# Two attention layers on one core: the third score before a block's first mixing, the last mixing after the seventh score, and 64 columns in the product of the row sums

## The chip, the cores and the metric

The kernel runs on one NeuronCore of a Trainium2 chip. The metric is the device time of one execution in microseconds. Four compute engines work side by side and are tied together by semaphores: TensorE (matrix products, PE in the profile), VectorE (DVE), ScalarE (ACT) and GpSimd (POOL). SyncE (SP) issues most of the transfers.

## The reference

The input is x of shape (8, 512, 32, 32): eight images of 512 channels and 1024 tokens. Two residual layers follow one another, each behind a group normalization; the second, the one touched here, mixes the heads before the softmax and normalizes the attention after it:

```python
attn = jnp.einsum('bhdq,bhdT->bhqT', q, k) * scale      # 8 heads, hd = 64
attn = jnp.einsum('gh,bhqT->bgqT', w_head, attn)        # mixing of the heads
attn = jax.nn.softmax(attn, axis=-1)
mean = jnp.mean(attn, axis=(-2, -1), keepdims=True)
var = jnp.var(attn, axis=(-2, -1), keepdims=True)
attn = (attn - mean) / jnp.sqrt(var + EPS)
attn = attn * in_gamma[None, :, None, None] + in_beta[None, :, None, None]
out = jnp.einsum('bhqT,bhdT->bhqd', attn, v)
```

All of it is in fp32.

## The kernel before, in words

The first layer runs for all eight images, then the second layer, one image after another (the loop `for b in range(B)`, line 1892). Only the second layer's class `Attention1` (from line 1616) is changed.

An image's 1024 queries are cut into eight blocks of 128; `p` counts them. For one block the work goes through five stages, each on another engine:

- **Scores** (`scores(p, i)`, line 1624), i from 0 to 7: four head pairs (`hp = i % 4`) for each half of the keys (`kh = i // 4`). Four matmuls on 64x64 tiles of the array fill one two-bank PSUM tile of the pool `ps1_m`; ScalarE (VectorE for odd i of block 0) copies it into the tile `raw[kh]`. The pool `rawpool` has two buffers, one for each half of the keys, so a block's first copy needs the buffer that the previous block's first half leaves.
- **Regrouping** (`regroup(kh, s)`, line 1645): two transfers of 256 KB on SP's queue carry a slice s of `raw[kh]` into the tile `re`, where all heads of a query lie next to each other on the partitions. `re` exists once, with four slices s; a slice is overwritten only when the mixing that reads it is done. The slices of a second key half need all of its four score copies, the eighth score's among them.
- **Mixing** (`mix(p, s)`, line 1658): sixteen matmuls on 32x32 tiles with the weights `wmix` fill two PSUM tiles of the same pool `ps1_m`. Two exponentials on ScalarE (line 1675), one for each tile, write the tile `e` (two buffers, pool `epool1`).
- **Transpose and moments** (`flip`, line 1680, `moments`, line 1692): VectorE transposes `e` into `et` and takes `bn` statistics of it. An `e` buffer is free when its moments are done.
- **Values** (`values(p, u, ...)`, line 1702): matmuls with `et` as the moving operand and 64 columns of `v` as weights on 128x64 tiles, four parts for each half u; `leave` (line 1722) copies the result out on ScalarE.

`sums` (line 1735) turns the `bn` statistics into the row sums and the sums of squares, `totals` (line 1745) adds them over partitions with two products against the selection matrix `sel`, and `reciprocals` (line 1755) goes on from there; it reads the first 32 rows of the result only.

The pool `ps1_m` has three buffers of two banks, which scores, mixings and projections take in turn; a group waits until the tile three places before it has been read. The values and the sums use the pool `ps1_a`, two buffers of one bank.

The order on each engine is the order in which the program calls its instructions (the schedule is set by hand, line 576). Per block there are four steps t (`step`, line 1838). In step t of block p the scores of block p, the mixing t of block p - 1 and values of block p - 2 (in step 3 of block p - 1) are interleaved. "First mixing" means `mix(p - 1, 0)`, in step 0; "last mixing" means `mix(p - 1, 3)`, in step 3. Step 8, after an image's last block, mixes block 7 and has no scores. Regroupings are issued at the end of a step: slices 0 and 1 of the first key half in step 1, slice 2 in step 2, slice 3 of the first half and then all four of the second half in step 3. An agenda (`ag.run`) places other work between: loads of the next image's input and weights (`piece`, `left_k`, `y` in the profile), its normalization at block 5, its projections in the last block.

Of the kernel before, what the change touches and what calls it, by code (L numbers as in the profile page):

```python
# [9 lines left out]
F32 = mybir.dt.float32  # L10
# [8 lines left out]
P = 128  # L19
# [448 lines left out]
def tile_two_attention_layers(  # L468
# [19 lines left out]
    nc = tc.nc  # L488
    B, C, T = x_d.shape
    H = w_head.shape[0]  # L490
    D = C // H
# [24 lines left out]
    def const_tile(name, shape, dt=F32):  # L516
        return const.tile(shape, dt, tag=name, name=name)
# [45 lines left out]
    sel = const_tile("sel", [P, 32])  # L563
# [130 lines left out]
    with ExitStack() as l0:  # L694
# [5 lines left out]
        stat = l0.enter_context(tc.tile_pool(name="stat", bufs=2))  # L700
# [368 lines left out]
        def attention0(b, agenda):  # L1069
# [96 lines left out]
            for i in range(0, NI + 2, 2):  # L1166
                if i < NI:
                    scores(i)
                    scores(i + 1)
                if i >= 2:  # L1170
                    for w in (i - 2, i - 1):
                        values(w)
                        sums(w)
                    if (i - 1) % NG == NG - 1:
                        g = (i - 1) // NG
                        agenda.at(i + 2, lambda g=g: totals(g))
                        agenda.at(i + 6, lambda g=g: reciprocals(g))
                        agenda.at(i + 10, lambda g=g: finish(g))
                agenda.run(i)
                agenda.run(i + 1)  # L1180
# [83 lines left out]
    with ExitStack() as l1:  # L1264
# [6 lines left out]
        stat = l1.enter_context(tc.tile_pool(name="stat1", bufs=2))  # L1271
# [5 lines left out]
        def acc_psum(nm):  # L1277
            return ps_a.tile([P, FB], F32, tag="a", name=nm)

        def m_psum(nm):  # L1280
            return ps_m.tile([P, 2, FB], F32, tag="m", name=nm)
# [163 lines left out]
        def k_leave():  # L1445
            for fn in due:
                fn()
            due.clear()
# [167 lines left out]
        class Attention1:  # L1616
# [41 lines left out]
            def mix(self, p, s):  # L1658

                b = self.b  # L1660
                ps = [m_psum(f"m1_{b}_{p}_{s}_{h}") for h in range(2)]
                for c in range(4):
                    for a in range(4):
                        rows = slice(a * 32, a * 32 + 32)
                        nc.tensor.matmul(  # L1665
                            ps[a // 2][c * 32 : c * 32 + 32, a % 2].rearrange(
                                "p (r kb k) -> p r kb k", r=2, k=32
                            ),
                            wmix[rows].rearrange("p g i -> p (g i)"),
                            re_t[rows, s].rearrange("p r (kb c k) -> p c r kb k", c=4, k=32)[:, c],  # L1670
                            start=True, stop=True, tile_position=(a * 32, c * 32),
                        )
                e = self.e[p, s] = epool.tile([P, 2, 4, 2 * P], F32, tag="e", name=f"e1_{b}_{p}_{s}")
                for h in range(2):
                    nc.scalar.activation(  # L1675
                        e[:, :, 2 * h : 2 * h + 2].rearrange("p r a k -> p a r k"),
                        ps[h].rearrange("p a (r k) -> p a r k", r=2), AF.Exp,
                    )

            def flip(self, p, s):  # L1680

                u, st = s // 2, s % 2
                if st == 0:
                    self.et[p, u] = etpool.tile(
                        [P, 8, 16, H, 4], F32, tag="et", name=f"et_{self.b}_{p}_{u}"
                    )
                nc.vector.transpose(  # L1687
                    self.et[p, u].rearrange("p kb (r st a) g q -> p st kb r (a g q)", r=2, st=2)[:, st],
                    self.e[p, s].rearrange("p r a (kb k) -> p kb (r a) k", k=32),
                )  # L1690
# [44 lines left out]
            def sums(self, p):  # L1735

                bn = self.bn.pop(p).rearrange("p s a (r k) -> p r (s a) k", k=3)
                zz = stat.tile([P, 2, 2, 16], F32, tag="zz", name=f"zz_{self.b}_{p}")
                mean, m2 = bn[..., 1], bn[..., 2]
                nc.vector.tensor_scalar_mul(zz[:, 0], mean, float(2 * P))  # L1740
                nc.vector.tensor_mul(zz[:, 1], mean, zz[:, 0])
                nc.vector.tensor_add(zz[:, 1], zz[:, 1], m2)
                self.zz = zz

            def totals(self, p):

                ps = acc_psum(f"z1_{self.b}_{p}")
                for m in range(2):
                    nc.tensor.matmul(
                        ps[:32, ts(m, 32)], self.zz[:, m].rearrange("p r c -> p (r c)"), sel,  # L1750
                        start=True, stop=True,
                    )
                self.reciprocals(p, ps)
# [84 lines left out]
            def step(self, p, t, ag):  # L1838

                new, old, older = p < NT, p >= 1, p >= 2  # L1840
                if t == 3 and old:
                    self.mix(p - 1, 3)
                if new:
                    self.scores(p, 2 * t)
                    if t == 0:
                        self.scores(p, 1)
                if t == 0 and older:
                    self.values(p - 2, 0, 2, 3)
                    self.leave(p - 2, 0)
                    self.sums(p - 2)  # L1850
                    if p % 2 == 0 and p >= 4:
                        self.divide(p // 2 - 2, nc.gpsimd)
                if t in (1, 2) and older:
                    self.values(p - 2, 1, t - 1)
                    if t == 1:
                        self.flip(p - 1, 0)
                        self.totals(p - 2)
                        self.moments(p - 1, 0)
                if t == 3 and old:
                    self.values(p - 1, 0, 0)  # L1860
                if new and t:
                    self.scores(p, 2 * t + 1)
                if t == 3 and old:
                    self.values(p - 1, 0, 1)
                if t < 3 and old:
                    self.mix(p - 1, t)
                ag.run(4 * p + t - 0.5)
                if t == 2 and older:
                    self.values(p - 2, 1, 2, 3)
                    self.leave(p - 2, 1)  # L1870
                k_leave()
                if p == 1 or old and t:
                    self.flip(p - 1, t)
                    self.moments(p - 1, t)
                if new:
                    for kh, s in (
                        (), ((0, 0), (0, 1)), ((0, 2),), ((0, 3), (1, 0), (1, 1), (1, 2), (1, 3)),
                    )[t]:
                        self.regroup(kh, s)
                if old and t == 0:  # L1880
                    self.piece(4 if p < 5 else 5)
                ag.run(4 * p + t)
# [155 lines left out]
```

## Time and profile before

| | us |
|---|---|
| median of three runs (4051.15 to 4058.64) | 4051.75 |
| the profiled execution | 4059.13 |
| its span, first to last instruction | 4057.0 |

| engine | busy us | share of the span |
|---|---|---|
| PE | 3927.5 | 97% |
| DVE | 2834.4 | 70% |
| ACT | 1969.0 | 49% |
| POOL | 128.7 | 3% |

The second layer's scores begin at 1800.6 us, and its last mixings end near 4000 us. The products of the row sums (line 1749) are 256 records of the form 128*32, in 64 groups; the mixings 8192 records of the form 32*32; the second layer's scores 4096 of the form 64*64; the values 16384 of the form 128*64. Each matmul of the program is two records. How to read it: a busy time is the sum of the durations of an engine's instructions, and a busy PE may still be waiting inside; idle time is laid to the releaser that came last by the semaphores, which can be another than the one named. Lines are those of the kernel before.

### The profile page before, as it was taken

The numbers are of one execution on the slowest core, as the hardware profiler recorded it, in microseconds if no ns is written. First come the engines' busy times: TensorE is split into PE (matmuls) and PEld (weight loads), VectorE is DVE, ScalarE is ACT, GpSimd is POOL, SyncE is SP. The second block draws the span as 40 slices with busy tenths as digits, with TensorE's granted clock in tenths as the row PEclk, the third lists the DMA queues.
The fourth block names the chain that finished last, engine by engine and source line by source line (L and its number), as shares of the span: only waits on it lengthen the run. The fifth ranks groups of instructions, "written<-read, shape, count | busy, mean of one in ns | idle before, by whom it ended". The sixth has DMA issues, their size and how long they took to land. (4 is left out here: it accounts for less than half of the span.)

```text
span 4057.0 us, 96037 instructions
## 1 busy us (share of the span) xinstructions
PE 3927.5 (97%) x41932; PEld 1817.7 (45%) x41932; DVE 2834.4 (70%) x4124; ACT 1969.0 (49%) x2431; POOL 128.7 (3%) x150
## 2 busy tenths in 40 slices
PE   8999999999999999999999999999999999999997
PEld 4353535353444435334444534544444444445344
DVE  4748475756666575748849859769679679498596
ACT  1727263545445363516617427347257166174273
POOL 0000000000000000000000001001000000000010
PEclk9999999999999999999999999999999999999998
DMA  3313131211111111228738639559469287386384
GB/s 124 114 47 115 45 118 48 87 50 59 60 66 66 68 53 60 77 83 208 182 120 220 189 105 234 155 143 231 128 174 233 78 216 194 114 223 193 104 212 121
DMA packets 268636, 519.12 MB, mean 128 GB/s; under 512 B 49840, under 2 KB 84912, under 8 KB 261552
## 3 DMA queue, kind: packets, MB, share of 16 engines
q1 hardware_dynamic: 261664, 497.96, 42.9%
q0 software_dynamic: 6544, 14.94, 1.6%
q8 instruction: 331, 5.42, 0.6%
q14 instruction: 97, 0.79, 0.1%
HBM read 197.16 MB, written 46.92 MB: 60 GB/s over the span
## 5 line engine op out<-in xcount | busy, mean ns | idle before, releaser
L1687 DVE STREAM_TRANSPOSE et<-e 128x2048 f32<-128x2048 f32 x256 | 586.7, 2292 | 133.8 <-ACT e L1675 127.6
L1714 PEld LDWEIGHTS a<-et,v 128*64 128x64 f32 x16384 | 509.4, 138 | 287.2 <-issue 215.8
L1698 DVE BATCH_NORM_STATS2 bn<-e 128x6 f32<-128x512 f32 x1024 | 633.5, 673 | 0.0
L1086 ACT ACTIVATE e<-s 128x1024 f32<-128x1024 f32 x512 | 497.2, 1026 | 233.9 <-PE s L1081 233.4
L1675 ACT ACTIVATE e<-m 128x1024 f32<-128x1024 f32 x512 | 496.3, 1021 | 208.4 <-issue 102.1
L1643 ACT COPY raw<-s 128x1024 f32<-128x1024 f32 x480 | 475.0, 1019 | 229.6 <-PE s L1631 193.1
L1714 PE MATMUL a<-et,v 128*64 128x64 f32 x16384 | 557.3, 225 | 5.8 <-DVE et L1687 5.1
L1631 PE MATMUL s<-k,q 64*64 64x512 f32 x4096 | 541.7, 615 | 9.7 <-DVE q L1497 3.1
L1094 DVE TENSOR_TENSOR zacc<-zacc,e 128x1024 f32<-128x1024 f32 x384 | 468.8, 1221 | 93.8 <-ACT e L1086 71.8
L1081 PE MATMUL s<-q,k 64*64 64x512 f32 x4096 | 490.1, 593 | 2.3 <-ACT e L1086 2.3
L1107 PE MATMUL a<-e,v 64*64 64x512 f32 x4096 | 484.1, 589 | 0.0
L1665 PE MATMUL m<-re,wmix 32*32 32x512 f32 x8192 | 334.9, 611 | 72.6 <-DMA re<-raw 60.7
L1107 PEld LDWEIGHTS a<-e,v 64*64 64x64 f32 x4096 | 156.7, 133 | 282.8 <-issue 282.5
L1081 PEld LDWEIGHTS s<-q,k 64*64 64x64 f32 x4096 | 147.9, 133 | 275.2 <-issue 240.7
L1631 PEld LDWEIGHTS s<-k,q 64*64 64x64 f32 x4096 | 118.0, 132 | 259.2 <-issue 85.0
L1458 PE MATMUL pv<-wv,y 128*128 128x512 f32 x480 | 212.1, 597 | 0.0
L1730 ACT COPY q<-a 64x256 f32<-64x256 f32 x256 | 93.7, 366 | 158.9 <-PE a L1714 156.3
L1665 PEld LDWEIGHTS m<-re,wmix 32*32 32x32 f32 x8192 | 71.6, 103 | 215.5 <-ACT raw L1643 88.3
L1763 POOL DMA_DIRECT2D zd<-rz x56 | 34.7, 619 | 3492.5 <-DMA y<-x 1858.2
L1458 PEld LDWEIGHTS pv<-wv,y 128*128 128x128 f32 x480 | 89.3, 190 | 117.4 <-issue 109.5
L1462 ACT COPY v<-pv 128x512 f32<-128x512 f32 x30 | 17.6, 585 | 218.4 <-PE pv L1458 218.4
L1092 DVE TENSOR_TENSOR zacc<-e,e 128x1024 f32<-128x1024 f32 x64 | 78.3, 1223 | 55.3 <-ACT e L1086 55.3
(315 smaller groups left out, 3936.8 us busy)
## 6 DMA issues: line engine op xcount, KB each, us to landing
re<-raw SPq DMA_DIRECT2D x1024, 256.0 KB
left_q<-left_q SPq DMA_DIRECT2D x17, 1792.0 KB
left_p<-left_p SPq DMA_DIRECT2D x17, 1792.0 KB
left_k<-left_k SPq DMA_DIRECT2D x10, 1792.0 KB
x<-in_x_dram SPq DMA_DIRECT2D x32, 512.0 KB
rzb<-zd SPq DMA_DIRECT2D x128, 128.0 KB
x<-x SPq DMA_DIRECT2D x64, 256.0 KB
left_v<-left_v SPq DMA_DIRECT2D x8, 1792.0 KB
```

Of the source, the lines that this page charges most:

```text
L1081: nc.tensor.matmul(ps[c * D : c * D + D, m], k[r, hp, k0 : k0 + D], q[r, hp, ts(f, FB)], start=True, stop=True,)
L1086: nc.scalar.activation(e[i], ps, AF.Exp, scale=S0 * S0)
L1094: nc.vector.tensor_add(zacc[g], zacc[g], e[i])
L1107: nc.tensor.matmul(acc[g][a][m * D : m * D + D], v[rows, kc, ts(2 * hp + m, D)], e[i][rows, m], start=(kc == 0), stop=(kc == NG - 1),)
L1458: nc.tensor.matmul(ps[:, m], y_t[b][:, c, ts(2 * i + m, P)], w[:, c], start=(c == 0), stop=(c == NCC - 1),)
L1631: nc.tensor.matmul(ps[c * D : c * D + D, m], qo_t[b][r, p, hp, ts(c, D)], k_t[b][r, hp, ts(kh, FB)], start=True, stop=True,)
L1643: nc.scalar.copy(dst, ps)
L1665: nc.tensor.matmul(ps[a // 2][c * 32 : c * 32 + 32, a % 2].rearrange("p (r kb k) -> p r kb k", r=2, k=32), wmix[rows].rearrange("p g i -> ...
L1675: nc.scalar.activation(e[:, :, 2 * h : 2 * h + 2].rearrange("p r a k -> p a r k"), ps[h].rearrange("p a (r k) -> p a r k", r=2), AF.Exp,)
L1687: nc.vector.transpose(self.et[p, u].rearrange("p kb (r st a) g q -> p st kb r (a g q)", r=2, st=2)[:, st], self.e[p, s].rearrange("p r a ( ...
L1698: nc.vector.bn_stats(self.bn[p][:, s, a], e[:, :, a].rearrange("p r k -> p k r"))
L1714: nc.tensor.matmul(acc[two * D : two * D + D, s].rearrange("p (x q) -> p x q", q=4), v_t[b][:, kb, ts(g, D)], et[:, kb, :, g], start=(kb = ...
```

## The change

Three things change in `Attention1`.

1. In `step`, the third score `scores(p, 2)` is called in step 0, right after the first two and ahead of the values, the output copies and the first mixing. In step 1 no score stands at the beginning any more.
2. In step 3, the seventh score `scores(p, 6)` is called before the last mixing, and no longer after it. The mixing issues its first exponential itself and hands back its second one, which step 3 calls after the eighth score (and its copy). In the other steps the second exponential follows at once, as before.
3. The tile `zz` gets a third part that repeats the first one. The two products of `totals` take two neighbouring parts as weights, 64 columns where there were 32, and write 64 rows of PSUM where they wrote 32; the additional rows are not read.

```diff
@@ mix @@
-                for h in range(2):
+
+                def exponentials(h):
                     nc.scalar.activation(
                         e[:, :, 2 * h : 2 * h + 2].rearrange("p r a k -> p a r k"),
                         ps[h].rearrange("p a (r k) -> p a r k", r=2), AF.Exp,
                     )
+
+                exponentials(0)
+                return lambda: exponentials(1)
@@ sums @@
-                zz = stat.tile([P, 2, 2, 16], F32, tag="zz", name=f"zz_{self.b}_{p}")
+                zz = stat.tile([P, 3, 2, 16], F32, tag="zz", name=f"zz_{self.b}_{p}")
                 mean, m2 = bn[..., 1], bn[..., 2]
-                nc.vector.tensor_scalar_mul(zz[:, 0], mean, float(2 * P))
+                nc.vector.tensor_scalar_mul(
+                    zz[:, 0::2], mean.unsqueeze(1).to_broadcast([P, 2, 2, 16]), float(2 * P)
+                )
@@ totals @@
-                        ps[:32, ts(m, 32)], self.zz[:, m].rearrange("p r c -> p (r c)"), sel,
+                        ps[:D, ts(m, 32)],
+                        self.zz[:, m : m + 2].rearrange("p m r c -> p (m r c)"), sel,
@@ step @@
-                if t == 3 and old:
-                    self.mix(p - 1, 3)
-                if new:
+                if new and t != 1:
                     self.scores(p, 2 * t)
                     if t == 0:
                         self.scores(p, 1)
+                        self.scores(p, 2)
+                if t == 3 and old:
+                    second = self.mix(p - 1, 3)
...
                 if new and t:
                     self.scores(p, 2 * t + 1)
                 if t == 3 and old:
+                    second()
                     self.values(p - 1, 0, 1)
                 if t < 3 and old:
-                    self.mix(p - 1, t)
+                    self.mix(p - 1, t)()
```

## The prediction

> **What bounds the kernel now.** I read the page first, then the waits of each engine from 1830 us on (the second layer, the only part touched), then the timeline of one query block. From the page:
>
> ```profile
> PE   3927.5 (97%) x41932; PEld 1817.7 (45%) x41932; DVE 2834.4 (70%) x4124; ACT 1969.0 (49%) x2431; POOL 128.7 (3%) x150
> ```
>
> TensorE is the bound, so what can be won is its idle time and the slots that its groups take. Waits, as engine, line, releaser, total us, times, longest:
>
> ```profile
> PE m L1665 <- DMA re<-raw: 60.7, 45, 4.4
> PE m L1665 <- ACT q L1730: 7.5, 9, 0.9
> ...
> ACT e L1675 <- DVE bn L1698: 38.8, 44, 2.0
> ```
>
> The idle time that matters is one place: the mixing waits for the regrouped scores (`re`). The timeline puts every one of these waits at a block's first mixing. Eight stand after an image's last block (2.63 to 4.39, sum 25.7), where no scores are left. Thirty-seven (35.0) stand between two blocks; the nine laid to `q` (7.5) and two more of 0.5 and 0.6 are the same place: 43.6 us over 48 intervals, 0.91 each. That it is not the `q` copy shows in other blocks, where the mixing starts before that copy ends.
>
> One interval, S being the eighth score (start us, us, engine, what):
>
> ```profile
> 3931.32 1.14 PE L1665 MATMUL m<-re,wmix 32*32 32x512 f32 x32
> 3932.39 1.10 PE L1631 MATMUL s<-k,q 64*64 64x512 f32 x8
> 3933.09 1.94 ACT L1675 ACTIVATE e<-m 128x1024 f32<-128x1024 f32 x2 [0.83 <-DVE bn L1698]
> 3934.51 1.09 PE L1631 MATMUL s<-k,q 64*64 64x512 f32 x8
> 3934.92 1.94 ACT L1643 COPY raw<-s 128x1024 f32<-128x1024 f32 x2
> 3936.61 1.95 PE L1631 MATMUL s<-k,q 64*64 64x512 f32 x16
> 3938.28 1.93 ACT L1643 COPY raw<-s 128x1024 f32<-128x1024 f32 x2 [1.42 <-PE s L1631]
> 3941.38 1.15 PE L1665 MATMUL m<-re,wmix 32*32 32x512 f32 x32 [0.81 <-ACT q L1730]
> 3942.46 1.09 PE L1631 MATMUL s<-k,q 64*64 64x512 f32 x8
> ...
> 3944.68 2.31 DVE L1687 STREAM_TRANSPOSE et<-e 128x2048 f32<-128x2048 f32 x1 [1.76 <-ACT e L1675]
> ```
>
> S = 3934.51. The eighth copy ends at S+2.36, and the first mixing (M) starts at S+6.87: 4.5 us from copy to landed data. PE's own work from S fills only 6.06. VectorE still idles 1.76 before its first transpose. Interval M to M: 21.93; without the wait 21.1.
>
> **What the skill says.** TensorEngine Tiling (Array Packing), Key Properties: a change of tiling mode drains TensorE. The trace agrees: two adjacent scores start 0.86 apart, while a score followed by another mode takes a slot of 1.02: 0.16 per change. Perfetto Trace Analysis, DMA Instruction — HWDGE: the semaphore follows a confirmed write, so there is delay after the last byte that no issue order shortens; the 4.5 us for two 256 KB copies agree. TensorE: Matmul & The Clock Gate, Part 1: idleness of about 3.4 us halves the clock. Here 2.21 us sufficed at 2237.95, where the clock reads 0.61 and then 0.54, and three slots took 4.8 us for 3.2.
>
> **The change, part by part.**
>
> *Third score before the first mixing.* It issues four matmuls (eight records) and one copy; no DMA, since regrouping stays in its step, so SP and POOL see nothing move. PE's work from S to M grows from 6.06 by 0.86 to 6.9. The data are due at S+6.7 (copy ending at S+2.2, below, plus 4.5), so the typical wait goes: minus 43.6. The score joins two others, and one mode change goes: 56 blocks x 0.16 = minus 9.0.
>
> Behind the moved copy on ScalarE stand the output copies (0.74) and then the first exponentials. The three copies start when the raw buffer is free, which needs the regroup of slice 3 landed. Today the copies start at S+3.25 to S+4.87, mean about 3.75. That regroup waits for the last mixing, which now ends about 1.0 later; I shift the copies by the whole of it, although a backlog of transfers may already set the landing. For a copy now at S+c: the second copy (whose PSUM the mixing takes) ends at S+c+3.0, the exponentials start at S+c+4.66. With M at S+7.25 (6.9 and the 0.28 below, rounded up) the first delays M where c > 4.25, the second the exponentials where c > 3.92 (they start 1.33 after M). Over the 48 values of c this gives 2.0 + 3.8: plus 6. The second mixing takes PSUM from these exponentials and has no slack left, so I count that lag in full.
>
> *Last mixing after the seventh score, second exponential after the eighth copy.* PE has as many mode changes as before. ScalarE's order becomes copy 7, exponential, copy 8, exponential. The exponentials wait for `bn` (an e buffer): today they start near S-1.4 and push copy 8 to S+2.36; then only one stands ahead, and copy 8 follows S directly, ending at S+2.17. The new wait: the second exponential ends at S+2.17+0.97 = 3.14, and the next block's second score takes its PSUM. PE would reach it at S+1.02+1.08+0.86 = 2.96, ScalarE releases it at about 3.24: 0.28 x 48 = plus 13.4. The fourth transpose waits for the same exponential; VectorE reaches it at S+3.0 today and nearer S+4 in the new order (S comes 1.02 sooner after M), so it costs nothing while `bn` covers it; uncovered, at most 0.2 per block.
>
> *Sums with 64 columns.* Values run as 128*64, the sums as 128*32: one mode change goes. No run shows this product at 64 columns. Ends: a full change saved, 64 x 0.16 = minus 10; or nothing saved and four wider weight loads at the values' 138 ns for 106, plus 0.03 x 4 x 64 = plus 8. I take 0.10 each, minus 6.4: the mode then equals its neighbour's. The VectorE product writes 64 elements instead of 32 (0.19 us now); 0.02 to 0.06 more, hidden in the idle 1.76 before the transpose.
>
> *What stays.* Three intervals wait 2.2 to 2.5, not by copy 8 but because the transfers are late (M at S+8.25, 8.27, 8.58): about 1.1 of each stays, plus 3.3. In seven images one interval carries normalisation, and VectorE has no idle time (M = 2521.99: no wait before the transpose); those cannot shorten by the full 0.6: plus 4. The eight waits after the last block stay. The half-clock stretch may vanish (1.6); not counted.
>
> Sum: -43.6 - 9.0 - 6.4 + 6 + 13.4 + 3.3 + 4 = -32.3. The profiled execution took 4059.1 (span 4057.0 and 2.1 around it), so 4027; the median of the runs shown is 7.4 below it: 4051.75 - 32 = 4020.
>
> **The rivals.**
>
> A. *Transfers bind.* In 2425 to 2560 us the DMA engines' share is 0.91, or 20.0 us per 21.95 us interval. In block 2206 they idle about 2 us while SP waits for copy 8; if that gap stays, nothing shortens by more than a few tenths. For it: six images carry extra loads in these blocks. Against it: the last image has a share of 0.82 to 0.87, and the same interval and wait, so latency sets it. Gain about 0.25 x 48 = 12: 4040, down to none.
>
> B. *The second exponential costs nothing* and the sums save all: 32 + 13 + 4 = 49 less: 4003.
>
> C. *Slower: copies pile up ahead of the exponentials.* If the slice-3 regroup lands much later than the shift I used, M waits for the second copy and the second mixing for the exponentials. An interval gains 0.91 + 0.26 - 0.28 = 0.89 before this. A copy at today's c = 4.9 costs 0.65 + 0.33, so the change decides to slower where the landings average 1.1 us beyond my shift. At 1.6 beyond (c = 5.35): 1.1 + 0.33 = 1.43, net 0.54 x 48 = 26 slower: 4078. For it: c reaches 4.87 today. Against it: the mean is 3.75.
>
> That nothing changes because the compiler's order is kept is excluded: the order is written out by hand.
>
> **How the numbers follow.** Forecast 0.58 (own range 4006 to 4034), A 0.19, B 0.12, C 0.11. A measurement of this kernel can tell 0.2%, 8 us. Of A, 0.07 falls within that of no change; faster is 0.58 + 0.12 + 0.12 = 0.82, slower C's 0.11. The range takes B's end and A without its weakest part: 4000 to 4046; outside it are C and some 0.07.
>
> **What would show it.** Right: first mixings between blocks without a wait of more than 0.3 typically; a new PE wait of score on `e` of 0.2 to 0.4 at a block's second score, some 48 times; copy 8 ending at S+2.2; sums in form 128*64; intervals near 21.3. A: those waits stay on DMA with the share at 0.95 or more. C: mixings wait on ACT `raw`, the second mixing on `e`, by over a microsecond. The prediction fails most easily in the 4.5 us from copy 8 to landed data, and in the landing of slice 3, both set by transfers that I can only shift, not derive.

## The result, and the profile after

The kernel after takes 4035.18 us (median; 4032.16 to 4037.43), the kernel before 4054.68 in the same comparison: a ratio of 0.9952 with an interval of 0.9937 to 0.9966, some 19 us faster. The forecast was 4020 with a range of 4000 to 4046: the sign was right, the gain less than two thirds of what was expected. The profiled execution after took 4037.07 (span 4035.0), the one before 4059.13 (span 4057.0).

The page of the kernel after, busy time of each engine:

```profile
PE 3929.8 (97%) x41932; PEld 1825.9 (45%) x41932; DVE 2836.2 (70%) x4124; ACT 1976.2 (49%) x2431; POOL 129.1 (3%) x150
```

TensorE is as busy as before while the span is 22 us shorter. A busy PE can wait inside its rows, as will be seen. The waits of TensorE from 1830 us on (releaser, total us, times, longest):

```profile
PE m L1665 <- DMA re<-raw: 30.7, 18, 3.5
PE z L1755 <- DVE zz L1748: 13.0, 17, 1.7
...
PE s L1631 <- ACT e L1676: 1.4, 8, 0.2
```

The mixing's wait for the regrouped scores was 60.7 in 45 places. Of the 30.7 left, eight waits behind each image's last block sum to 22.5 (2.6 to 3.5 each, as I expected them to stay); only 8.2 stand between blocks, where there were 43.6 with those laid to `q`. In its place has come a wait that was not on the list before: the sums' product waits 13.0 for the sums that VectorE makes. The third score used to stand between the first mixing and that product; now TensorE comes to the product sooner. The wait that I had predicted, a score on the second exponential, is not there: 1.4 in all. Of ScalarE's own waits, the exponentials' wait for `bn` fell from 38.8. The copies' waits on transfers need a closer look:

```profile
ACT e L1676 <- DVE bn L1702: 17.0, 16, 2.1
ACT raw L1643 <- DMA re<-raw: 13.0, 18, 1.2
ACT raw L1643 <- DMA y<-x: 5.7, 8, 1.0
ACT raw L1643 <- DMA left_k<-left_k: 4.8, 5, 1.4
```

A score copy waits for its buffer `raw`, which is free when the transfers that read it are done. The second of these lines is no newcomer; it was longer before:

```profile
ACT raw L1643 <- DMA re<-raw: 27.6, 20, 2.3
```

Nearly all of it, before and after, belongs to a block's first copy (27.4 before, 11.0 after). The newcomer shows when the copies are told apart by their score (worked out from the timelines of ScalarE): the fifth score's copy, the first of a second key half, waited 2.4 us before and waits 17.2 after. The profile lays only 2.0 of this to `re<-raw`, 10.5 to loads that use the same queue (`y`, `left_k`) and 4.7 to nothing that it shows ("issue"), so that it is the buffer is a reading, which the experiments test. One interval in the timeline (S = 3916.50 is the eighth score, M = 3923.35 the first mixing):

```profile
3909.16 1.93 ACT L1643 COPY raw<-s 128x1024 f32<-128x1024 f32 x2 [0.70 <-issue]
3909.50 1.86 PE L1665 MATMUL m<-re,wmix 32*32 32x512 f32 x32
...
3916.50 1.09 PE L1631 MATMUL s<-k,q 64*64 64x512 f32 x8
3917.66 1.01 ACT L1643 COPY raw<-s 128x1024 f32<-128x1024 f32 x1 [0.96 <-PE s L1631]
3918.56 1.04 ACT L1676 ACTIVATE e<-m 128x1024 f32<-128x1024 f32 x1
3918.60 2.81 PE L1631 MATMUL s<-k,q 64*64 64x512 f32 x24
3920.74 2.84 ACT L1643 COPY raw<-s 128x1024 f32<-128x1024 f32 x3 [1.14 <-PE s L1631]
3923.35 1.14 PE L1665 MATMUL m<-re,wmix 32*32 32x512 f32 x32
3925.47 0.39 PE L1755 MATMUL z<-sel,zz 128*64 128x32 f32 x4
```

The eighth copy ends at S+2.17, the first mixing starts unwaited at S+6.85, and three scores stand together in 2.81. The first two rows shown are the fifth and sixth copies and the third mixing of the interval before: the copies start 0.70 late, and the mixing takes 1.86, so TensorE waits inside it. The same two in the kernel before, where the copy had no wait:

```profile
3927.06 1.02 ACT L1643 COPY raw<-s 128x1024 f32<-128x1024 f32 x1
3928.22 1.16 PE L1665 MATMUL m<-re,wmix 32*32 32x512 f32 x32
```

To see where the gain went I took the start of every TensorE group in the 40 intervals between blocks 2 and 7 of all images and averaged the distances (worked out from the timelines; us):

```
stretch                                        before   after   change
the three scores (separately / together)        2.92     2.74    -0.18
last values to first mixing (its wait)          2.96     2.29    -0.68
values to sums' product                         1.08     1.37    +0.28
sums' product to fourth score                   0.24     0.31    +0.07
third mixing to next group                      1.34     1.66    +0.32
everything else                                13.77    13.80    +0.03
interval                                       22.33    22.17    -0.16
```

The two gains that I forecast are there, the mode change in full and the wait in good part. Three quarters of them are given back within the same interval: at the sums' product and inside the third mixing. So these 40 intervals bring only 6.4 of the 22.0 us by which the span is shorter. More, 9.3, comes from eight intervals that I had not looked at apart, from the first mixing of an image's block 1 to that of block 2: 21.40 before, 20.23 after. No sums' product stands there, and the wait (8.4 us in eight places) is saved whole. The rest, 6.3, lies at the image ends and in front of the second layer. (The interval from block 7 to step 8's first mixing fell from 22.47 to 21.65, but only because its third score, a slot of 1.02, now stands ahead of it.) At these ends the profiled executions of all kernels, before and after, scatter by as much as this rest, so I don't lay it to the change.

### The profile page after: what moved, and what is told of

Read it like the earlier page. It is cut to its first block, busy times and chain, and to the rows that moved or that the text cites. A ratio compares the mean times of both kernels' runs of the same rounds, so it can differ in the third digit from the quotient of the medians.

```text
span 4035.0 us, 95990 instructions
## 1 busy us (share of the span) xinstructions
PE 3929.8 (97%) x41932; PEld 1825.9 (45%) x41932; DVE 2836.2 (70%) x4124; ACT 1976.2 (49%) x2431; POOL 129.1 (3%) x150
## 5 line engine op out<-in xcount | busy, mean ns | idle before, releaser
L1631 PE MATMUL s<-k,q 64*64 64x512 f32 x4096 | 523.8, 608 | 8.0 <-DVE q L1497 3.1
L1665 PE MATMUL m<-re,wmix 32*32 32x512 f32 x8192 | 352.8, 606 | 36.8 <-DMA re<-raw 30.7
```

Source lines behind the costliest of these rows:

```text
L1631: nc.tensor.matmul(ps[c * D : c * D + D, m], qo_t[b][r, p, hp, ts(c, D)], k_t[b][r, hp, ts(kh, FB)], start=True, stop=True,)
L1665: nc.tensor.matmul(ps[a // 2][c * 32 : c * 32 + 32, a % 2].rearrange("p (r kb k) -> p r kb k", r=2, k=32), wmix[rows].rearrange("p g i -> ...
```

## The experiments

Three theories of what sets the interval now. T1: the bytes of the transfers. T2: VectorE, whose late sums hold TensorE. T3: the way from the eighth copy over its eight transfers to the two places that wait for them, the first mixing (data) and, through the freed buffer, the copy of the fifth score. Times are medians; differences to the kernel before are given by the ratio to it, in us at 4055, and so are differences to the kernel after (its own ratio is 0.9952). Single executions of one kernel scatter by some 5 us, so medians decide on times and traces only on mechanisms.

### Third score alone

```
-                if new:
+                if new and t != 1:
                     self.scores(p, 2 * t)
                     if t == 0:
                         self.scores(p, 1)
+                        self.scores(p, 2)
```

> The third score alone moves before the first mixing; last mixing and sums as before. The prediction's own sum without the other two parts: 43.6 of waits and 9.0 of mode changes gone, some 9 left or new: about 43 us faster. Theory T1 (once the first mixing no longer waits, the transfers set the interval, so order on the engines hardly matters): 10 to 20 us faster, as much as the whole change. Theory T2 (the first mixing comes sooner, so the row sums' product, and with it TensorE, waits for VectorE's zz): the product waits for zz 15 times or more, 10 us or more in all.

Measured: 4059.01, ratio 1.0009 (1.0 to 1.0017): no gain, which none of the three had expected. Waits of TensorE and ScalarE in this kernel:

```profile
PE m L1665 <- DMA re<-raw: 37.2, 33, 4.0
PE s L1631 <- ACT e L1675: 10.6, 24, 0.7
```

```profile
ACT e L1675 <- DVE bn L1698: 65.0, 54, 2.0
```

Most of the first mixing's waits between blocks go, as hoped (12.2 left of 43.6), but the exponentials now wait 65.0 us for VectorE's `bn` (38.8 before), with the seventh and eighth copies queued behind them; a score waits for the exponentials, and the third mixing's stretch grows from 1.34 to 1.85. The product waits for the sums only 3.8 us in 8 places, less than T2 asked for. The profiled execution is the fastest of twelve (4051.33); what holds the typical one back by 8 us more, it can't show.

### Last mixing alone

```
-                if t == 3 and old:
-                    self.mix(p - 1, 3)
                 if new:
                     self.scores(p, 2 * t)
...
+                if t == 3 and old:
+                    second = self.mix(p - 1, 3)
...
                     self.scores(p, 2 * t + 1)
                 if t == 3 and old:
+                    second()
```

> The last mixing after the seventh score with the late second exponential, alone. The prediction's sum: the eighth copy 0.15 us earlier, 7 us off the first mixing's waits, against 13 us of a second score that waits for the second exponential: 6 us slower. The trace of the whole change showed no such wait of the second score (three scores in 2.73 us), so I now expect 5 to 10 us faster or nothing; both theories: no waits of the product for zz, since the first mixing isn't sooner.

Measured: 4051.38, ratio 0.9992 (0.9984 to 1.0): some 3 us, between 0 and 6. The exponentials' wait on `bn` falls to 4.7, and still the mixing waits 60.4 us for its data in 47 places, nearly as long as before (60.7): between S and M TensorE has only its 6.06 us of work, less than the data take to come.

### Sums with 64 columns alone

```
-                zz = stat.tile([P, 2, 2, 16], F32, tag="zz", name=f"zz_{self.b}_{p}")
+                zz = stat.tile([P, 3, 2, 16], F32, tag="zz", name=f"zz_{self.b}_{p}")
...
-                        ps[:32, ts(m, 32)], self.zz[:, m].rearrange("p r c -> p (r c)"), sel,
+                        ps[:D, ts(m, 32)],
+                        self.zz[:, m : m + 2].rearrange("p m r c -> p (m r c)"), sel,
```

> The 64 columns alone. The prediction: 6.4 us faster, ends 10 faster and 8 slower. From the slots in the trace of the whole change (values to product 0.98 instead of 1.08, product to score 0.31 instead of 0.24) 0.03 us per block: 2 us faster, not to be told from none.

Measured: 4052.22, ratio 0.9991 (0.9982 to 0.9999), some 4 us, not to be told from the 2 or the 6 that were expected. The slots show less: values to product 1.08 to 1.00, product to the next score 0.24 to 0.30, a net 0.02. The full mode change saved at the entry returns in good part at the exit.

### Third score and last mixing, without the 64 columns

The kernel after with the former `sums` and `totals`.

> The change without the 64 columns. The prediction's sum: 26 us faster than before, 6 less than with them. T1: as the whole change, 20 us faster. T2: the product waits for zz about as often as in the whole change (17 times, 13 us), since the columns have nothing to do with it.

Measured: 4041.46, ratio 0.9964 (0.9952 to 0.9976): 15 us faster, where the two alone gave +4 and -3. Each takes away what the other is stopped by. The third score gives TensorE 0.86 us of work to cover the transfers but leaves the eighth copy behind two exponentials that wait for `bn`; the last mixing's new place gets the copy out early but leaves nothing to cover the transfers. Together the mixing's waits are 37.7 in 22 places, and `bn` 16.6. The intervals from block 1 to block 2 show this most plainly, since all eight of a kernel are nearly alike. There the eighth copy ends at S+2.55 before, at S+2.68 with the third score alone and at S+2.17 with the last mixing moved, alone or with the third score; the interval takes 21.40 before, 21.62 and 21.05 with one part alone, and 20.25 with both. In the 40 later intervals the third score alone already brings 22.16, as short as with both (22.14), so there the profiled executions don't show the interaction. The product waits for the sums 6.8 us in 21 places, half of what T2 asked for. That the three parts give 19 together is within the intervals of 15 and 4.

### The next image's loads left out, before and after

```
-                a.pieces += [lambda i=i: y_piece(b + 1, i) for i in range(4 * NCC)]
-                a.pieces += [lambda i=i: left_piece(("k", b + 1), i) for i in range(14)]
+                if b == 0:
...
+                else:
+                    y_t[b + 1], w_t["k", b + 1] = y_t[b], w_t["q", b]
```

> The kernel before without the loads of the next image's input and key weights during the blocks, for images 1 to 6 (image 0 keeps them); it leaves out these 30 loads of 128 KB per image, 4 to 5 per block, and computes with what lies in the tiles, so its output isn't the reference's. T1 (bytes: the DMA engines' total work sets the interval): some of the first mixing's wait goes, 0 to 15 us faster than before. T3 (the latency from the eighth copy over its eight regroup transfers, which stand ahead of these loads in the queue, sets it): no change. Its use is as the base of the next run.

> The changed kernel without the same loads (leaves out the same part). T1: an interval falls from 22.15 to about 21.5 as in image 7 of the changed kernel, which has few such loads (129.5 us for six intervals instead of 133): 36 intervals x 0.6 = 20 us less than the changed kernel, so 40 us under before and 25 to 35 under the kernel before without loads. T3: as the changed kernel, 20 us under before.

Measured: before without them 4056.7, ratio 1.0000 (0.9991 to 1.0009); after without them 4026.85, 0.9923 (0.9907 to 0.994). The loads cost the kernel before nothing and the kernel after some 8 to 12 us: its 40 intervals fall to 21.88 and the third mixing's stretch from 1.66 to 1.42, with the fifth score's copy waiting 5.1 us instead of 17.2. Transfers have come closer to being the bound, but the whole gain of some 30 lies between what T1 and T3 asked for, and this run by itself decides neither way.

### The sums' product late

```
                         self.flip(p - 1, 0)
-                        self.totals(p - 2)
                         self.moments(p - 1, 0)
+                    else:
+                        self.totals(p - 2)
```

> The changed kernel with the product of the row sums one step later (after the second part of the values in step 2), so that it never waits for zz. T2 (VectorE's zz is the new bound): 8 to 13 us less than the changed kernel, the sum of these waits. T1 and T3: at most 3 us less; the wait turns up at the third mixing or the first instead.

> The same with 32 columns as before. The prediction: 6 us more than with 64. From the slots (0.03 us per block): 2 us more, not to be told from none.

Measured: 4092.21, ratio 1.0088 (1.0071 to 1.0105), and with 32 columns 4092.41, 1.0089 (1.0063 to 1.0114). No wait for the sums is left, and the kernel is some 55 us slower than after (57 by the medians). The product is no end in itself: the reciprocals that follow from it are sent to DRAM and read back to all partitions, 256 KB on POOL's queue. In the timeline of the kernel with 64 columns, where S is 3940.60:

```profile
3942.12 0.54 POOL L1777 DMA_DIRECT2D rzb<-zd  x1 [2.15 <-DMA zd<-rz]
...
3948.97 1.15 PE L1665 MATMUL m<-re,wmix 32*32 32x512 f32 x32 [1.45 <-DMA re<-raw]
```

The broadcast now goes out as the eighth copy's transfers do, and the first mixing comes at S+8.37 instead of S+6.85. The mixing waits 48 times for its data, 88.2 us in all, 57.5 more than after; the values wait a further 9.7 us for a PSUM tile that the late reciprocals still read. The eighth copy ends at S+2.17 as in the kernel after, but the first mixing between blocks comes 5.94 us behind it on average instead of 4.93. That is about what 256 KB take at 250 GB/s, 1.0 us (an estimate from the slices below); no run leaves the broadcast out, so this is the likely cause and not an isolated one. A loss of this size was in no expectation. It speaks for T3, sharpened: what counts is what else the transfer engines do in the few microseconds behind the eighth copy. In the kernel after, the slices of that stretch (length; busy time of PE, PEld, DVE, ACT, POOL; clock, DMA share, GB/s) are full:

```profile
3918.00:3920.00 2.00, 2.00 (x40) 1.10 (x39) 2.00 (x5) 1.60 (x2) 1.85 (x1) 1.00 0.58 174
3920.00:3922.00 2.00, 2.00 (x38) 0.91 (x32) 2.00 (x1) 1.26 (x2) 0.00 (x0) 1.00 0.97 245
3922.00:3924.00 2.00, 2.00 (x82) 1.51 (x76) 2.00 (x5) 1.99 (x4) 0.00 (x0) 1.00 1.05 257
3924.00:3926.00 2.00, 2.00 (x66) 1.53 (x44) 1.22 (x4) 1.52 (x3) 0.00 (x0) 1.00 1.01 244
```

So the eight transfers of the second half (2.1 MB) would take some 8.5 us at 244 to 257 GB/s (an estimate), in one burst, and the slice ahead of it, in which the engines are busy to 0.58 only, helps nobody.

### Both exponentials at once

The kernel after with `self.mix(p - 1, 3)()` and without `second()`.

> The kernel after, with both exponentials of the last mixing directly behind it, as before the change; the last mixing still follows the seventh score. ScalarE then does the second exponential (1.04 us) ahead of the copy of the eighth score instead of behind it. If the early copy of the eighth score is what lets the first mixing start unwaited (the transfers behind it run with all DMA engines busy, so each microsecond that they start later is one that they end later), the copy ends 0.5 to 1.0 us later, the wait of the first mixing on the transfers comes back with 0.3 to 0.8 us in each of the 48 intervals: 4045 to 4070 us, waits of the mixing on the transfers 45 to 70 us instead of 30.7. If the gain came from the place of the last mixing alone and the deferral does nothing: 4035, within 3, waits as in the kernel after.

Measured: 4044.95, ratio 0.9973 (0.9963 to 0.9983): the deferral is worth some 8 to 10 us, at the lower end of what was expected, and only in part for the reason given. In the eight intervals from block 1 to block 2 it is that reason: the eighth copy ends at S+2.65 instead of S+2.17, the first mixing waits again, and the interval takes 20.81 instead of 20.23, 4.6 us in all. In the 40 later ones the copy ends at S+2.20 on average, and they are no longer than after (22.10 against 22.17). The mixing's waits rise only to 39.4. What else differs in the trace is that the data land later behind the copy at an image's end: behind an image's last block, where nothing covers them, the first mixing starts 6.1 to 6.2 us after the eighth copy's end in four of eight images, 4.5 to 4.9 in the others; in the kernel after it is 4.5 to 5.4 in all eight. But this is no mark of the missing deferral: the kernel with both moves and 32 columns defers too and shows 6.1 to 6.2 three times. Why the backlog is longer in some image ends stays open. The same kernel shows the other waiting place well:

```profile
3919.07 1.93 ACT L1643 COPY raw<-s 128x1024 f32<-128x1024 f32 x2 [0.57 <-DMA re<-raw]
...
3919.54 1.74 PE L1665 MATMUL m<-re,wmix 32*32 32x512 f32 x32
```

The copy of the fifth score waits for a transfer of the burst to let go of the buffer, and the third mixing, which needs the PSUM tile that this copy reads, takes 1.74 instead of 1.16.

### The sums' product one score later

```
                         self.flip(p - 1, 0)
+                        if new:
+                            self.scores(p, 3)
                         self.totals(p - 2)
                         self.moments(p - 1, 0)
...
-                if new and t:
+                if new and t and (t != 1 or not older):
                     self.scores(p, 2 * t + 1)
```

> The kernel after, with the sums' product moved behind the fourth score (it stood between the first part of the second values and the fourth score), so that TensorE reaches it some 1.0 us later; the order on VectorE is as it was. If the late sums on VectorE are a bound of their own, the 13.0 us of waits of the product on them fall to under 3 and the time by about 10: 4025. If VectorE's lateness only passes on (the reciprocal, then the moments behind it, then the exponentials' buffers), the waits go, others come up in their place, and the time stays within 4 of 4035. If the reciprocals' transfers, issued 1.0 us later, fall into the burst of the regrouping transfers as they did when the product was moved by 4 us (which cost 57), a quarter of that: 4045 to 4050.

Measured: 4036.19, ratio 0.9954 (0.9938 to 0.997): the same as after. The wait for the sums goes:

```profile
PE z L1755 <- DVE zz L1748: 1.9, 4, 0.8
```

It was 13.0. But the third mixing's stretch grows from 1.66 to 1.92 and the waits of the fifth score's copy from 17.2 to 21.6. T2 falls as a bound of its own: time saved at the sums is spent at the next gate.

### The last two transfers left out

```
-                        self.regroup(kh, s)
+                        if p == 0 or (kh, s) != (1, 3):
+                            self.regroup(kh, s)
```

> The kernel after, leaving out for every pair of heads but an image's first the last two of the eight transfers of the second half of the scores (heads 3 and 7), 0.5 MB of some 5.0 MB in an interval, so that stale scores are mixed there. At the 245 to 257 GB/s that the burst shows, the eight transfers (2.1 MB) then end about 2.1 us sooner, and so does the release of the buffer that the copy of the fifth score waits for. If that release is what holds the third mixing (the slot up to the next values takes 1.66 us on average, 1.34 before the change), the slot falls to 1.35 or less and the intervals by 0.3: 4020, with under 2 us of the 13.0 left in the copies' waits on transfers. If the DMA engines' total bytes bind the interval, it falls by up to 2 us until TensorE's own 20.85 binds: 3975 to 3985. If VectorE's late sums are the bound, the slot shortens but the waits for the sums grow by as much: 4032 to 4037.

Measured: 4024.48, ratio 0.9927 (0.991 to 0.9944), 10 us under after. The third mixing's stretch falls to 1.27, below its value before the change, and the 40 intervals to 21.73; the waits for the sums hardly move:

```profile
PE z L1755 <- DVE zz L1748: 14.3, 23, 1.8
```

A tenth of the bytes less took 0.4 off the interval, not 2: total bytes (T1) don't bind. The slot that answers is the one behind the buffer's release, by as much as T3 said. The copies' waits on transfers read 19.9 (single waits up to 5.0), not under 2; but all of these are a block's first copies, and the fifth score's copy, the one meant, has none left. The exponentials' wait for `bn` is longer here than after (27.3 against 17.0), so a late second exponential ahead of that copy is not what stretched the third mixing. Over the runs the two go together: waits of the fifth score's copy of 0, 2.4, 5.1, 17.2 and 21.6 us (this run, before, loads left out, after, product a score later) stand beside third-mixing stretches of 1.27, 1.34, 1.42, 1.66 and 1.92; the other kernels fit in between.

### The loads moved

```
-                if old and t == 0:
-                    self.piece(4 if p < 5 else 5)
+                if old and t == 2:
+                    self.piece(5)
```

> The kernel after, with the next image's loads (128 KB each, on SP's queue) issued five at a time in the third quarter of a block, behind the regrouping of head 2, instead of four or five in the first quarter, behind the burst of the eight second-half transfers. They then fall into the stretch of some 6 us between the third mixing and the eighth score's copy, in which the DMA engines' share is 0.57 to 0.69 in four of the 2 us slices, and no longer lengthen the stretch in which the engines are at 0.97 to 1.05. If what the loads cost is their place in that burst, this keeps most of the 8 to 10 us that leaving them out saved: 4027 to 4031. If their bytes cost the same wherever they are, nothing changes: 4035, within 3. If they push the transfers of head 3, and with them the copy into the other buffer or the burst itself, later by a microsecond or more in the six blocks that have them, waits of the first mixing come back: 4045 or more.

Measured: 4107.62, ratio 1.0119 (1.0102 to 1.0136): some 68 us slower than after (72 by the medians), far beyond the worst that I had set down. From the timeline of an interval with loads (the first row is the copies of the next block's first three scores):

```profile
1903.04 2.84 ACT L1643 COPY raw<-s 128x1024 f32<-128x1024 f32 x3 [2.80 <-DMA re<-raw]
1905.29 1.15 PE L1665 MATMUL m<-re,wmix 32*32 32x512 f32 x32 [1.22 <-ACT raw L1643]
```

SP's queue issues the loads from 1892.77 to 1896.77, ahead of slice 3's transfers and of the burst. Slice 3's transfers of the first key half free the buffer for the next block's first copies, which now start at S+6.69 on average instead of S+4.08, 2.6 us later: as long as the 0.66 MB of five loads take at 250 GB/s (an estimate). Issuing them also keeps SP busy for 4 us; no run separates the two. The first mixing takes PSUM from the second of these copies and waits. In all, first mixings wait 77.4 us for data and 33.4 for copies. The third mixing's stretch is at 1.29 and the sums' wait at 1.2: with the first gate late, the later ones are free. The last image has no next image to load for, only eight other loads in its first two blocks; its six intervals from block 2 on take 129.1 us, against 129.5 after. So the loss comes with the loads, and since at their old place they cost 8 to 12, it is their place that costs.

No variant is faster than the kernel after with its whole computation; the one with the product a score later equals it.

## Why the prediction was right, point by point

The measured time lies well inside the range, but that is partly luck: a cost that didn't come (13.4) and two that the sum lacked or had too small (24 us where it had 4) offset each other in part, and the interval of 21.3 that I named as a sign was not reached (21.85 over 48 intervals, 22.17 before).

*First-mixing waits (minus 43.6, plus 3.3 that stay).* Right in the mechanism: 8.2 us of waits between blocks is left (and 0.8 laid to `q`), of 43.6, some 6 more than I counted. The data came as derived, the eighth copy at S+2.17 (predicted 2.2) and the first mixing at S+6.87 in the typical block, 7.1 on average.

*Third score's mode change (minus 9.0).* Right: the three scores take 2.74 in place of 2.92, 0.18 for each block instead of 0.16. (The 0.86 is the distance from a second score to a third; a first and a second start 0.91 apart.) But neither this nor the waits paid by themselves: alone, the third score gained nothing. My sum added the parts as if each stood by itself. It had the interaction in it only in that copy 8 at S+2.2 came from the other edit.

*Copies and exponentials behind the third copy (plus 6).* Too much: I shifted the first copies by the whole microsecond by which the last mixing ends later. Over the 48 intervals they start at S+4.03 on average, against S+3.76 before, so the backlog of transfers had set much of their start already, as I had allowed; no first mixing waits for a copy. Rival C's mechanism, copies late enough that the mixing waits for them, is real: moving the loads brought it about, at S+6.69.

*Second score waits for the second exponential (plus 13.4).* Wrong: nothing. The three scores run 2.81, just 0.86 more than two. The exponential starts at S+2.06, before the copy's row ends, and ends at S+3.10, while TensorE comes to the second score near S+3.0; the 0.28 was a difference of sums of durations from two engines, and neighbouring rows of ScalarE overlap by 0.1, which the sum left out. Rival B named this, and got it right for this term alone.

*Sums with 64 columns (minus 6.4).* The median alone gives some 4 (0.4 to 7), the slots 1. The entry saves 0.08 as I took it to, but the exit pays 0.06, which I left out.

*VectorE's full intervals (plus 4).* Far too small, and in the wrong place: the stretch to the sums' product grew by 0.28 per interval, 11 us in 40 intervals. I looked for what a full VectorE would do only where normalization runs, and not at what the third score had covered at its old place: VectorE's way to the sums.

*What the sum didn't have.* The third mixing: plus 0.32 per interval, 13 us in 40. I had followed the transfers of the second half to their data, the first mixing, and not to their other end, the buffer that they free for the fifth score's copy. Leaving the last two transfers out brought that stretch to 1.27 and the time down by 10. Had the sum contained these two gates with their measured size (11 and 13) and no second-exponential term, it would have read -32.3 - 13.4 - 4 + 24 = -25.7 instead of -32.3, and 4026 in place of 4020; with the waits that are really left (8.9 instead of 3.3) it reads -20.1. The median gain is 19.5. The terms for the copies and for the 64 columns are off by 6 and by 2 to 5, in opposite directions.

*The rivals.* A (transfers bind, 4040) came nearest in time, and is half right: not by their total, since leaving out a tenth of the bytes gave 0.4 of a possible 2 us, but by the burst. Its sign, first mixings that go on waiting for DMA, didn't show. C's slower kernel didn't come.

## What to carry to other kernels

When a wait for data is covered, follow the same transfers to their other end: the buffer that they release has a waiter too, and it is next in line. Edits that shorten two sides of one handover (more work on the waiting engine, an earlier producer) are not to be summed; each alone gave next to nothing here (+4 and -3 us), both together -15. And a transfer that has plenty of slack for its own reader, a broadcast or a prefetch, is not free to move: what it costs depends on whether it falls into a burst that someone waits for.

## What the runs showed of the hardware

The burst: three 2 us slices in a row with the DMA engines' share at 0.97 or more carried 244 to 257 GB/s in the kernel after. A full share is no fixed rate: the slice from 3696 to 3698 us, which holds no regrouping, carried 430 GB/s at a share of 1.03. Two edits that only moved where 0.26 and 0.66 MB of other transfers fall cost some 55 and 68 us; by the estimates above, what waits behind them came later by about their size over 250 GB/s.

The clock: in the kernel after, TensorE waits 2.6 to 3.5 us behind each image's last block. In the seven images with a successor the stretch from that mixing to step 8's last mixing takes 20.0 to 20.2 us five times and 18.50 twice. Slices of one of the slow ones, after a wait of 2.62 us:

```profile
3686.00:3688.00 2.00, 2.00 (x33) 0.63 (x31) 1.74 (x6) 0.69 (x1) 0.00 (x0) 0.68 1.04 242
3688.00:3690.00 2.00, 2.00 (x4) 0.79 (x3) 1.97 (x2) 1.25 (x2) 0.00 (x0) 0.50 1.08 247
```

The clock (third column from the end) is granted at 0.68 and 0.50, and eight records of a projection take 5.16 us for 3.70. After a wait of 2.61 us at 2554.19 it stayed at 1.00 and they took 3.70:

```profile
2554.00:2556.00 2.00, 1.81 (x34) 0.76 (x35) 2.00 (x4) 0.47 (x1) 0.00 (x0) 1.00 1.04 245
2556.00:2558.00 2.00, 2.00 (x6) 0.81 (x6) 1.74 (x5) 1.46 (x2) 0.00 (x0) 1.00 1.08 248
```

The other short stretch, with the clock at 1.00 too, follows a wait of 2.92. So an idle stretch of that length can cost a further 1.6 us or none; its length alone doesn't tell which. TensorE: Matmul & The Clock Gate, Part 1, of the Trainium skill has about 3.4 us for this; here 2.6 was enough.
